# Query and key projections of two chunks by seven quarter products (Winograd's form of Strassen's scheme) in an attention kernel on one core

## The chip, the cores and the metric

The kernel runs on one core of one Trainium2 chip. The metric is the device time of one execution in microseconds; the median of the runs is given. A core has five engines with a queue each: TensorE (PE, matrix products; its weight loads are listed as PEld), VectorE (DVE), ScalarE (ACT), GpSimd (POOL) and SyncE (SP, which here only issues DMAs). An engine works through its queue in order and waits at an instruction whose semaphores aren't there yet. [...]

## The reference

The input is `x`, 4 batches of 1024 tokens with 512 features. It is normalised over its features and goes through an attention layer with 16 heads of 128 and through a product with rounding to FP8; both are added to `x`. Shortened:

```python
xn = layernorm(x)
q  = rope(rmsnorm(heads(xn @ Wq + bq), qn_w))
w  = softmax((xn @ Wcmp + bcmp) in groups of 4 tokens)
entries = weighted sums of xn over each group          # 256 per batch
ck = rope(rmsnorm(entries @ Wk + bk, kn_w));  cv = entries @ Wv + bv
sc = where(causal, q @ ck.T / sqrt(128), NEG)
ctx_sparse = softmax over the 8 largest of sc, times cv
lk = rope(rmsnorm(heads(xn @ Wlk + blk), kn_w));  lv = heads(xn @ Wlv + blv)
ctx_local = softmax(banded q @ [lk of the previous 128, lk of these 128].T) @ [lv, lv]
attn = ((ctx_sparse + ctx_local) / 2) @ Wo + bo
ffn  = (fp8(xn / 2) * 2) @ (fp8(input2 / 2) * 2)
out  = x + attn + ffn
```

All products but the FP8 one are fp32, and an fp32 product appears as two instructions with two weight loads.

## The kernel before, in words

The tokens are cut into NT = 32 chunks of 128 (eight per batch), the heads into NU = 8 pairs. A **unit** is one chunk with one pair of heads, so there are NN = 256 units, and unit `n` is chunk `n // 8`, pair `n % 8` (`place`). All weights stay in SBUF: `wqk_sb[u]` holds 256 query and 256 key columns of a pair, `wlv_sb[u]` the value columns, `wo_sb[u]` the rows of Wo.

The order of the instructions is written out by hand (`manual_schedule`): the main loop runs over `s`, and one turn of it does different stages of several units, so that each engine's queue has work of other units in front of what would have to wait:

- `queries(s+3)`: four products of 128x512 (K = 512 in four tiles; L606) give queries and keys in one PSUM bank, `qp`. Two banks alternate.
- `squares` and `spread`: ACT sums the squares of the four heads from `qp` (L321), POOL makes the reciprocal roots (L315, L316).
- `normalize(s+2)`: DVE multiplies `qp` by them and by the norm's weights into `th` (L634). `rotate` turns half of each head: one product on POOL (L337), one product, one subtraction and one addition on DVE (L339, L341, L342).
- `turn_keys(s+2)` and `fetch_keys(s+2)`: DVE transposes in 32x32 blocks (L687, L690), SP writes the result to DRAM in four DMAs (L695) and reads it back, turned, as `qT` and `lkT` (L705).
- `scores(s)`: q against the keys of the previous chunk, of this chunk and of the compressed entries (L754, L761, L764) into `sc`.
- `weigh(s)`: DVE masks and finds maxima (L786, L800), the eight largest (L807), the negated maximum of them (L809) and marks them (L812); ACT takes exponentials (L814, L822).
- `settle(s)`: DVE keeps the marked ones and sums (L830), bounds the sums from below (L839) and inverts them (L840); `divide(s)`: ACT multiplies (L847).
- `turn(s)`, `fetch(s)`: DVE transposes the probabilities (`probB`, L865), SP writes them to DRAM in one DMA (`pr`, L873) and reads them back in four (`probT`, L907).
- `values_of(s+1)` and `keep_values`: four products of 128x256 (L712), copied by ACT (`lv`, L724).
- `values(s-1)`: the probabilities against the values (L924); `keep_context(s-2)`: ACT copies them out (L939); `to_output(s-2)`: two products with `wo_sb` (L957) into a bank that sums a chunk's eight units; after the eighth DVE adds it to the chunk (L966) and SP stores it.

On PE a turn is: scores(s), queries(s+3), to_output(s-2), values_of(s+1), values(s-1). SP's queue holds in a turn: the write of `pr`, four writes of keys, four reads of `probT`, two reads of `qT` and `lkT`, and then what chunks need.

Work that belongs to a chunk is done in small steps within the turns: `chunk_prep` (layer norm, transposed tokens to DRAM, group weights and sums), `fetch_tokens` and `fetch_with_ones` (tokens back, turned; row 0 of the first K-tile is replaced by ones so that the bias comes with the product), `chunk_entries` (the compressed keys and values), `chunk_eight` with `quantize` (rounding on DVE and POOL, L287 to L298, and the FP8 product L588). The first eight units turn keys and probabilities on PE.

PSUM: two banks `qp`, two `sc`, two `pp` (values, FP8 product, entries), one `ctx`, one `out`.

Of the kernel before, what the change touches and what calls it, by code (L numbers as in the profile page):

```python
# [19 lines left out]
P = 128  # L20
# [18 lines left out]
def kernel(  # L39
# [34 lines left out]
    NN = NT * NU  # L74
    assert S // RATIO <= 2 * P and NU == 8 and HID == 512
# [10 lines left out]
    def scratch(name, shape=(P, 512), dtype=F32):  # L86
        return work.tile(list(shape), dtype, tag="scratch", name=name, bufs=2)

    def pp(name):
        return psum.tile([P, 512], F32, tag="pp", name=name, bufs=2)  # L90
# [5 lines left out]
    x_tiles, angles = {}, {}  # L96

    def load_x(t, purpose, extra=False):

        b, c = divmod(t, NCH)  # L100
        if extra:
            xt = scratch(f"x_{purpose}_{t}")
        else:
            xt = work.tile([P, HID], F32, tag="x", name=f"x_{purpose}_{t}")
        nc.sync.dma_start(xt, hidden[b, ts(c, P), :])
        x_tiles[purpose, t] = xt

    def load_angles(t):
        c = t % NCH
        cs = work.tile([P, ROPE], F32, tag="cs", name=f"cs_{t}")  # L110
        nc.sync.dma_start(cs, rope[ts(c, P), :])
        angles[t] = cs
# [10 lines left out]
    wqk_sb = [const.tile([P, KK, 512], F32, name=f"wqk_{u}") for u in range(NU)]  # L123
    wlv_sb = [const.tile([P, KK, 256], F32, name=f"wlv_{u}") for u in range(NU)]
    wo_sb = [const.tile([P, 2, HID], F32, name=f"wo_{u}") for u in range(NU)]

    def load_wqk(u, engine):
        for i, w in enumerate((Wq, Wlk)):
            engine.dma_start(
                wqk_sb[u][:, :, ts(i, 256)], w[:, ts(u, 256)].rearrange("(k p) n -> p k n", p=P)  # L130
            )
# [4 lines left out]
    def load_wo(u, engine):  # L136
        engine.dma_start(wo_sb[u], Wo[ts(u, 256), :].rearrange("(h p) n -> p h n", p=P))
# [13 lines left out]
    for k in range(KK):  # L151
        for i, w in enumerate((Wq, Wlk)):
            nc.sync.dma_start(wqk_sb[0][:, k, ts(i, 256)], w[ts(k, P), 0:256])
# [109 lines left out]
    def fold_first_row(u):  # L263
        w = wqk_sb[u]
        row = first_row.pop(u, None)
        if row is None:
# [3 lines left out]
                row, ident[:, 0:1].to_broadcast([P, P]), w[:, 0, :], start=True, stop=True  # L270
            )
        nc.vector.tensor_tensor(
            w, w, row.unsqueeze(1).to_broadcast([P, KK, 512]), ALU.subtract
        )
        for i, bias in enumerate((bq, blk)):
            nc.sync.dma_start(
                w[0:1, 0, ts(i, 256)], bias[ts(u, 256)].partition_broadcast(1)
            )

# [21 lines left out]
    w2_sb = const.tile([P, KK, HID], BF16, name="w2_sb")  # L301


    w2_raw = [wo_sb[NU // 2 + k][:, 0, :] for k in range(KK)]

    def round_w2():
        for k in range(KK):
            spare = wo_sb[NU // 2 + k][:, 1, :]
# [14 lines left out]
    def rotate(th, cs, nh, a, name, bb=None):  # L323
# [17 lines left out]
        nc.vector.tensor_tensor(x12[:, :, 0, :], a[:, :, 0, :], bb[:, :, 1, :], ALU.subtract)  # L341
        nc.vector.tensor_tensor(x12[:, :, 1, :], a[:, :, 1, :], bb[:, :, 0, :], ALU.add)  # L342


    GC = P // NE
    entries = {}
# [4 lines left out]
    def chunk_prep(t):  # L351
# [46 lines left out]
        log = work.tile([P, 1], F32, tag="log", name=f"log_{t}", bufs=1)  # L398
        row = work.tile([P, 2, BLK], F32, tag="row", name=f"row_{t}", bufs=1)
        red = work.tile([P, BLK // RATIO], F32, tag="red", name=f"red_{t}", bufs=1)  # L400
# [19 lines left out]
        if not t:  # L420
            add_tokens_here(row)
            return
# [21 lines left out]
        else:  # L444
            stores.append((pooled[g][i], few))
        yield "added"
# [31 lines left out]
    def turn_tokens_here(xt):  # L478
# [4 lines left out]
        xnT = work.tile([P, KK, P], F32, tag="xnT", name="xnT_0")  # L483
# [3 lines left out]
    def fetch_tokens(t):  # L487
        xnT = work.tile([P, KK, P], F32, tag="xnT", name=f"xnT_{t}")
# [5 lines left out]
        chunks[t] = xnT, xones[t % 2]  # L494


    xones = [const.tile([P, P], F32, name=f"xone_{i}") for i in range(2)]

    def fetch_with_ones(t):
        turned = tokens.pop(t).rearrange("i (b k) a j -> b i k (a j)", b=NB)  # L500
        for b in range(NB):
            lo = 0 if b else 1
            nc.sync.dma_start(
                xones[t % 2][b * BLK + lo : (b + 1) * BLK], turned[b, lo:, 0, :]
# [92 lines left out]
    def place(n):  # L597

        return divmod(n, NU)

    def queries(n):
        t, u = place(n)
        xnT, xone = chunks[t]
        qp = psum.tile([P, 512], F32, tag="qp", name=f"qp_{n}")
        for k in range(KK):
            nc.tensor.matmul(  # L606
                qp,
                xnT[:, k, :] if k or not t else xone,
                wqk_sb[u][:, k, :],
# [7 lines left out]
        ss = work.tile([P, 4], F32, tag="ss", name=f"ss_{n}")  # L617
        units[n] = {"qp": qp, "ss": ss}

    def squares(n, heads):  # L620
        w = units[n]
        for i in heads:
            square_sum(w["ss"][:, i : i + 1], w["qp"][:, ts(i, D)], f"{n}_{i}")
# [5 lines left out]
    def normalize(n):  # L629
        w = units[n]  # L630
        qp, r = w.pop("qp"), w["r"]
        th = work.tile([P, 4, D], F32, tag="th", name=f"th_{n}", bufs=1)
        for i in range(4):
            nc.vector.scalar_tensor_tensor(  # L634
                th[:, i, :],
                qp[:, ts(i, D)],
# [22 lines left out]
    def turn_keys_here(n):  # L659
# [4 lines left out]
        for i in range(4):  # L664
            nc.tensor.transpose(tq[:, ts(i, P)], th[:, i, :], ident)

# [7 lines left out]
    def key_tiles(n):  # L674
        w = units[n]
        qT = work.tile([P, NB, 2 * BLK], F32, tag="qT", name=f"qT_{n}", bufs=2)
        lkT = work.tile([P, NB, 2 * BLK], F32, tag="lkT", name=f"lkT_{n}", bufs=NU + 2)
# [3 lines left out]
    def turn_keys(n):  # L681
# [10 lines left out]
        )  # L692
        turned = dram.tile([NB, NB, BLK, 4 * BLK], F32, tag="qk", name=f"qk_{n}")
# [13 lines left out]
    def values_of(n):  # L707
        t, u = place(n)
        xnT = chunks[t][0]
        vp = pp(f"vp_{n}")  # L710
        for k in range(KK):
            nc.tensor.matmul(  # L712
                vp[:, 0:256],
# [7 lines left out]
    def keep_values(n):  # L721
        w = units[n]
        lv = work.tile([P, 2, D], F32, tag="lv", name=f"lv_{n}", bufs=NU + 2)
        nc.scalar.copy(lv.rearrange("p h d -> p (h d)"), w.pop("vp")[:, 0:256])  # L724
# [12 lines left out]
    def scores(n, h):  # L737
# [6 lines left out]
        if n == NN - 2:  # L744

            w.setdefault("sc", []).append(psum.tile([P, 512], F32, tag="qp", name=f"sc_{n}_{h}"))
# [6 lines left out]
        if c:  # L753
# [3 lines left out]
                units[n - NU]["lkT"][:, :, ds(h * BLK, BLK)],  # L757
# [6 lines left out]
        nc.tensor.matmul(sc[:, spa], q, ckT[:, 0:m], start=True, stop=True)  # L764
# [451 lines left out]
```

## Time and profile before

| | |
|---|---|
| median of 3 runs | 2642.6 us (2640.92 to 2643.14) |
| span of the profiled execution | 2641.7 us |
| PE busy | 2609.3 us, 11879 instructions |
| DVE busy | 2213.4 us, 8381 instructions |
| ACT busy | 1390.9 us, 5560 instructions |
| POOL busy | 786.2 us, 1128 instructions |
| DMA | 422.20 MB, 722252 packets |
| granted TensorE clock, mean | 0.999 |

The span reaches from the first to the last instruction of the profiled execution; the runs are timed without a profile. Busy times are the union of an engine's instructions; since products are pipelined and their ends are modelled, the distance from one start to the next says more about PE than the duration of one. A "releaser" is the instruction or DMA whose semaphore ended a wait. Some of the costliest groups (busy us, mean ns of one, idle time before them and what ended it):

```profile
L606 PE MATMUL qp<-wqk,xnT 128*128 128x512 f32 x1552 | 709.8, 593 | 3.0 <-DMA wqk<-in_L_attn_Wlk_dram 2.4
...
L847 ACT ACTIVATE prob<-prob,tot 128x256 f32<-128x256 f32 (+7 forms) x1024 | 382.0, 443 | 294.5 <-DVE tot L840 294.5
...
L957 PE MATMUL op<-wo,cT 128*128 128x512 f32 x1024 | 481.6, 593 | 4.2 <-ACT cT L939 4.2
L712 PE MATMUL vp<-wlv,xnT 128*128 128x256 f32 x2048 | 483.6, 379 | 0.0
...
L865 DVE STREAM_TRANSPOSE probB<-prob 128x512 f32<-128x512 f32 (+2 forms) x490 | 305.8, 629 | 11.5
...
L924 PE MATMUL cp<-probT,lv 128*128 128x128 f32 x1920 | 299.0, 276 | 6.4 <-DMA probT<-pr 4.9
```

### The profile page before, as it was taken

The page shows a single profiled execution, that of the slowest core. Times are in us where ns is not written, and L with a number is a line of the kernel's source. Part 1 is how long each engine was busy: PE and PEld are TensorE (multiplying, and loading weights), DVE is VectorE, ACT ScalarE, POOL GpSimd, SP SyncE. Part 2 cuts the span into 40 slices and gives each one's busy share as a digit, 9 for nine tenths or more (in the row PEclk, how much of TensorE's full clock was granted, in tenths as well). Part 3 has the DMA queues.
Part 4 walks back from the last instruction along what each step waited for, and adds up shares of the span by engine and source line. Part 5 has one row for each costly group of instructions (what it writes and reads, how often), then busy time and mean ns, then how long its engine had stood idle before and what let it go on. Part 6 is the DMA issues. An engine that isn't in the chain of part 4 may idle for free.

```text
span 2641.7 us, 46868 instructions
## 1 busy us (share of the span) xinstructions
PE 2609.3 (99%) x11879; PEld 1784.3 (68%) x11879; DVE 2213.4 (84%) x8381; ACT 1390.9 (53%) x5560; POOL 786.2 (30%) x1128
## 2 busy tenths in 40 slices
PE   8999999999999999999999999999999999999998
PEld 4666666776666666767766666667666666676776
DVE  6888888889888888888888888888888888877886
ACT  3545545555555555555555555555555555555555
POOL 3522323223332223232233322233323322322222
PEclk9999999999999999999999999999999999999999
DMA  8356556666655555666655555666665555566554
GB/s 255 110 156 162 151 145 175 171 176 158 164 143 154 162 155 156 169 173 170 166 157 144 158 149 158 177 164 164 171 176 147 150 148 153 147 168 171 159 152 110
DMA packets 722252, 422.20 MB, mean 160 GB/s; under 512 B 395823, under 2 KB 671552, under 8 KB 721984
## 3 DMA queue, kind: packets, MB, share of 16 engines
q1 hardware_dynamic: 721952, 419.20, 58.8%
q8 instruction: 97, 1.59, 0.3%
q14 instruction: 171, 1.40, 0.2%
q10 hardware_dynamic: 32, 0.02, 0.0%
HBM read 225.80 MB, written 193.20 MB: 159 GB/s over the span
## 4 chain that ended last, share of the span: by engine, by line
PE 84%; DVE 7%; ACT 3%; DMA 3%; SPq 2%; issue 1%; POOL 0%; ACTq 0%; DVEq 0%
PE qp L606 28%; PE op L957 14%; PE vp L712 14%; PE cp L924 13%; PE sc L764 5%; PE sc L761 4%; PE sc L754 4%; ACT prob L847 1%; ACT prob L814 1%; PE fp L588 1%; DVE sc L786 1%; DVE probB L865 1%; PE ep L536 1%; SPq L695 1%; DVE taken L812 1%
## 5 line engine op out<-in xcount | busy, mean ns | idle before, releaser
L606 PE MATMUL qp<-wqk,xnT 128*128 128x512 f32 x1552 | 709.8, 593 | 3.0 <-DMA wqk<-in_L_attn_Wlk_dram 2.4
L814 ACT ACTIVATE prob<-sc,neg 128x256 f32<-128x256 f32 (+1 forms) x512 | 235.9, 461 | 773.3 <-DVE taken L812 744.0
L606 PEld LDWEIGHTS qp<-wqk,xnT 128*128 128x128 f32 x1552 | 295.0, 190 | 372.5 <-issue 368.8
L847 ACT ACTIVATE prob<-prob,tot 128x256 f32<-128x256 f32 (+7 forms) x1024 | 382.0, 443 | 294.5 <-DVE tot L840 294.5
L712 PEld LDWEIGHTS vp<-wlv,xnT 128*128 128x128 f32 x2048 | 389.0, 190 | 161.3 <-issue 116.2
L957 PE MATMUL op<-wo,cT 128*128 128x512 f32 x1024 | 481.6, 593 | 4.2 <-ACT cT L939 4.2
L712 PE MATMUL vp<-wlv,xnT 128*128 128x256 f32 x2048 | 483.6, 379 | 0.0
L337 POOL TENSOR_TENSOR rb<-th,cs 128x256 f32<-128x256 f32 x256 | 203.8, 796 | 740.0 <-DVE th L634 733.2
L786 DVE CUSTOM_DVE_ANT_0 sc<-sc,mask_b 128x256 f32<-128x256 f32 (+1 forms) x512 | 211.6, 414 | 172.7 <-PE sc L764 162.7
L957 PEld LDWEIGHTS op<-wo,cT 128*128 128x128 f32 x1024 | 193.6, 190 | 229.8 <-issue 186.8
L865 DVE STREAM_TRANSPOSE probB<-prob 128x512 f32<-128x512 f32 (+2 forms) x490 | 305.8, 629 | 11.5
L315 POOL TENSOR_SCALAR r<-ss 128x4 f32<-128x4 f32 x256 | 61.9, 242 | 843.3 <-ACT junk L321 840.6
L924 PE MATMUL cp<-probT,lv 128*128 128x128 f32 x1920 | 299.0, 276 | 6.4 <-DMA probT<-pr 4.9
L321 ACT ACTIVATE junk<-qp 128x128 bf16<-128x128 f32 x1024 | 278.6, 272 | 28.9 <-PE qp L614 4.5
L924 PEld LDWEIGHTS cp<-probT,lv 128*128 128x128 f32 x1920 | 272.8, 191 | 25.4 <-issue 9.3
L634 DVE SCALAR_TENSOR_TENSOR th<-qp,r,norm_w 128x128 f32<-128x128 f32 x1024 | 286.1, 342 | 0.7 <-POOL r L316 0.4
L316 POOL TENSOR_TENSOR r<-r,nhalf 128x4 f32<-128x4 f32 x256 | 265.6, 1037 | 21.4
L830 DVE SCALAR_TENSOR_TENSOR prob<-taken,prob 128x128 f32<-128x128 bf16 (+7 forms) x512 | 186.4, 365 | 98.1 <-ACT prob L822 96.6
L606 PE MATMUL qp<-wqk,xone 128*128 128x512 f32 x496 | 258.3, 602 | 0.9 <-DMA xone<-xb_dram 0.7
L924 PE MATMUL cp<-probT,cv 128*128 128x128 f32 x1536 | 255.1, 275 | 0.0
L764 PE MATMUL sc<-ckT,qT 128*128 128x96 f32 (+7 forms) x1024 | 226.4, 303 | 0.0
L924 PEld LDWEIGHTS cp<-probT,cv 128*128 128x128 f32 x1536 | 212.7, 192 | 0.0
(141 smaller groups left out, 3674.9 us busy)
## 6 DMA issues: line engine op xcount, KB each, us to landing
pr<-probB SPq DMA_DIRECT2D x125, 512.0 KB
probT<-pr SPq DMA_DIRECT2D x500, 128.0 KB
qk<-thb SPq DMA_DIRECT2D x992, 64.0 KB
pr<-probB SPq DMA_DIRECT2D x96, 384.0 KB
probT<-pr SPq DMA_DIRECT2D x384, 96.0 KB
qT<-qk SPq DMA_DIRECT2D x248, 128.0 KB
lkT<-qk SPq DMA_DIRECT2D x248, 128.0 KB
x_norm<-_attn_hidden_states_dram SPq DMA_DIRECT2D x32, 256.0 KB
```

Of the source, the lines that this page charges most:

```text
L316: nc.gpsimd.tensor_tensor(r, r, nhalf[: ss.shape[0], 0:n], ALU.pow)
L321: nc.scalar.activation(junk[: src.shape[0]], src, AF.Square, accum_out=acc)
L606: nc.tensor.matmul(qp, xnT[:, k, :] if k or not t else xone, wqk_sb[u][:, k, :], start=(k == 0), stop=(t > 0 and k == KK - 1),)
L634: nc.vector.scalar_tensor_tensor(th[:, i, :], qp[:, ts(i, D)], r[:, i : i + 1], norm_w[:, i // 2, :], ALU.mult, ALU.mult,)
L712: nc.tensor.matmul(vp[:, 0:256], xnT[:, k, :], wlv_sb[u][:, k, :], start=(k == 0), stop=(k == KK - 1),)
L764: nc.tensor.matmul(sc[:, spa], q, ckT[:, 0:m], start=True, stop=True)
L786: nc.vector.tensor_tensor_reduce(sc[h][:, loc], sc[h][:, loc], mask_b[:, loc], -1.0, TAKEN, ALU.add, ALU.min, neg[h][0],)
L814: nc.scalar.activation(probs[h][:, loc], sc[h][:, loc], AF.Exp, bias=neg[h][0], scale=-1.0, accum_out=tot[:, h, 0:1],)
L847: nc.scalar.mul(probs[h][:, cols], probs[h][:, cols], tot[:, h, part : part + 1])
L865: nc.vector.transpose(pb[:, :, ds(h * g, g), :], prob[:, parts[0] * P : (parts[-1] + 1) * P].rearrange("p (g b i) -> p b g i", b=NB, i=BLK),)
L924: nc.tensor.matmul(blocks(cp[:, h, :]), v, probT[:, :, h * len(parts) + i - parts[0], :], start=(i == parts[0]), stop=(i == parts[-1]),)
L957: nc.tensor.matmul(op, cT[:, h, :], wo_sb[u][:, h, :], start=(u == 0 and h == 0), stop=(u == NU - 1 and h == 1),)
```

## The change

From chunk 4 on (unit FIRST = 32) chunks are taken in pairs: units alternate between the two chunks of a pair, with the same pair of heads, so that unit `2q` and `2q+1` use the same weights. Their queries and keys are a product of two chunks by 512 features with 512 features by (256 query + 256 key columns). Each side is cut in 2 x 2 quarters, A by chunk and half of K, B by half of K and queries or keys, and the four quarters of the result come from seven products of quarters instead of eight. A product of quarters (`product`) is two K-tiles of 128x256.

- **Combined weights**: four differences of weight quarters for each pair of heads are made once, by POOL, in units 9 to 24 (`combine_weights`), and stored in DRAM. For each pair of units they are loaded again, four DMAs of 256 KB (`load_combined`), into the places in SBUF of a quarter of the weights that is no longer used.
- **Sums of tokens**: four sums per pair of chunks on POOL (`sum_tokens`).
- **Products**: p1, p6, p5 and p3 go into one PSUM region, one after the other, each adding to what stands there; between them ACT copies the state out into `th` (`keep1`, `keep6`, `keep5`, `keep3`). p2 goes to another bank, p7 and p4 to a third, where p4 is added to p7. DVE adds p2, p7 and p7 + p4 to parts of `th` (`sum2`, `sum7`, `sum4`). Even turns hold p1, p2, p6, p7, odd ones p5, p3, p4. Squares and normalisation read `th` (SBUF) from then on, not PSUM.
- **Room**: the `wo` rows are loaded for each unit, later for each pair of units (512 KB), into two buffers; `lkT`, `lv`, `th` and the token tiles come from hand-managed pools; the value products and the context share one bank; FP8 products and entries share the bank of p2. `to_output` moves ahead of `settle` in program order, on PE between p2 or p5 and the next product.
- **Vector work**: the two additions of the rotation go from DVE to POOL; the negated maxima of both heads are made by one instruction instead of two; the lower bound of the sums (L839) is left out but for the first chunk of a batch.
- Steps of chunk preparation, entries, FP8 products and loads of tokens get new turns. In `values` the rows of entries that don't exist yet are left out.

The diff, cut to its core:

```diff
+    combined = [
+        dram.tile([4, P, 512], F32, tag=f"combined_{u}", name=f"combined_{u}", bufs=1)
+        for u in range(NU)
+    ]
+    def combine_weights():
+        one, two = (v.rearrange("p h d -> p (h d)") for v in th_tiles[2:])
+        for u in range(NU):
+            (b11, b12), (b21, b22) = (
+                [flat(wqk_sb[u][:, j, i]) for i in range(2)] for j in range(2)
+            )
+            for i, (to, a, b) in enumerate(
+                ((one, b12, b11), (two, b22, one), (one, b21, two), (two, b22, b12))
+            ):
+                nc.gpsimd.tensor_tensor(to, a, b, ALU.subtract)
+                stores.append((combined[u][(0, 1, 3, 2)[i]], to))
+                yield
+    def load_combined(q, which):
+        for i in which:
+            at = ring[(4 * (q - FIRST // 2) + (2, 0, 1, 3)[i]) % len(ring)]
+            nc.sync.dma_start(at, combined[q % NU][i])
+            loaded[q, i] = at.rearrange("p (k n) -> p k n", k=2)
+    def sum_tokens(p):
+        (a11, a12), (a21, a22) = ((b[:, 0:3:2, :], b[:, 3:5, :]) for b in (x_bufs(2 * p), x_bufs(2 * p + 1)))
+        s1, s2, s3, s4 = token_sums
+        op = nc.gpsimd.tensor_tensor
+        op(s1, a21, a22, ALU.add)
+        op(s2, s1, a11, ALU.subtract)
+        op(s3, a11, a21, ALU.subtract)
+        op(s4, a12, s2, ALU.subtract)
...
-        nc.vector.tensor_tensor(x12[:, :, 0, :], a[:, :, 0, :], bb[:, :, 1, :], ALU.subtract)
-        nc.vector.tensor_tensor(x12[:, :, 1, :], a[:, :, 1, :], bb[:, :, 0, :], ALU.add)
+        adder = nc.gpsimd if nh > 1 else nc.vector
+        adder.tensor_tensor(x12[:, :, 0, :], a[:, :, 0, :], bb[:, :, 1, :], ALU.subtract)
+        adder.tensor_tensor(x12[:, :, 1, :], a[:, :, 1, :], bb[:, :, 0, :], ALU.add)
...
+    regions = [v[:, 0:256] for v in (qk_banks[0], pp_bank, qk_banks[1])]
+    def product(i, a, b, first=True):
+        for k in range(2):
+            nc.tensor.matmul(regions[i], a[k], b[:, k, :],
+                start=first and k == 0, stop=k == 1, skip_group_check=not first)
+    def p1(q):
+        p, u = divmod(q, NU)
+        xa, one = chunks[2 * p]
+        product(0, (one, xa[:, 1, :]), wqk_sb[u][:, 0, 0])
+    def keep1(q):
+        take_th(2 * q)
+        nc.scalar.copy(half(2 * q, 0), regions[0])
+    def p2(q):
+        product(1, both(chunks[2 * p][0][:, 2:4, :]), wqk_sb[u][:, 1, 0])
+    def p6(q):
+        product(0, both(token_sums[1]), loaded.pop((q, 1)), False)
+    def p7(q):
+        product(2, both(token_sums[2]), loaded.pop((q, 2)))
+    def p5(q):
+        product(0, both(token_sums[0]), loaded.pop((q, 0)), False)
+    def p3(q):
+        product(0, both(token_sums[3]), wqk_sb[u][:, 1, 1], False)
+    def p4(q):
+        product(2, both(chunks[2 * p + 1][0][:, 2:4, :]), loaded.pop((q, 3)), False)
+    def add_to(n, i, what):
+        nc.vector.tensor_tensor(half(n, i), half(n, i), what, ALU.add)
...
         for_unit(s, (scores, 0), (scores, 1))
         for_unit(s - 2, (keep_context,))
+        if odd:
+            for_pair(q, (p5,), (keep5,))
+        elif s != FIRST - 4:
+            for_pair(q, (p1,), (keep1,), (p2,))
         for_unit(s, (weigh,))
-        for_unit(s + 3, (queries,))
+        if s + 3 < FIRST:
+            for_unit(s + 3, (queries,))
+        if even:
+            for_pair(q + 1, (load_combined, (1, 2)))
+        else:
+            for_pair(q + 1, (load_combined, (0, 3)))
+        for_pair(*((q, (sum7,)) if odd else (q - 1, (sum4,))))
         for_unit(s + 2, (normalize,))
+        for_unit(s - 2, (to_output,))
+        if even:
+            for_pair(q, (p6,), (keep6,))
         for_unit(s, (settle,))
         for_unit(s, (divide,))
         for_unit(s + 2, (go_on_rotating,), (end_rotation,))
+        if even:
+            for_pair(q, (sum2,))
+        for_unit(s + 1, (values_of,))
+        if odd:
+            for_pair(q, (p3,), (keep3,))
         if by_dma(s):
             turn(s)
         for_unit(s + 3, (squares, (0, 1, 2, 3)), (spread,))
-        for_unit(s - 2, (to_output,))
-        for_unit(s + 1, (values_of,))
         for_unit(s - 1, (values,))
+        for_pair(q, (p4 if odd else p7,))
```

## Prediction

> **What bounds the kernel now.** I read the engine table first, then the chain of waits in a stretch of ordinary units, then PE's weight loads, the waits, and the DVE and SP timelines of the same stretch.
>
> ```profile
> span 2641.7 us, 46868 instructions
> ...
> PE 2609.3 (99%) x11879; PEld 1784.3 (68%) x11879; DVE 2213.4 (84%) x8381; ACT 1390.9 (53%) x5560; POOL 786.2 (30%) x1128
> ...
> q1 hardware_dynamic: 721952, 419.20, 58.8%
> ```
>
> PE is never without work, but DVE at 84% is close behind it, and the DMA engines are 59% taken. The chain of waits shows what a unit is made of (start, us, what):
>
> ```profile
> 1514.56 3.46 PE qp L606 x8
> 1518.02 1.72 PE op L957 x4
> 1519.74 1.73 PE vp L712 x8
> 1521.46 1.34 PE cp L924 x12
> 1522.80 0.24 PE sc L754 x2
> ...
> 1524.19 3.46 PE qp L606 x8
> ```
>
> One unit after the other is on the chain with PE alone: 3.46 + 1.72 + 1.73 + 1.34 and 1.38 for scores are 9.63 us, and every eighth unit has 0.86 for the FP8 product (L588). An fp32 product is two instructions, so the x8 are four products. A 512-wide instruction takes 3.46/8 = 0.43 us, a 256-wide one 1.73/8 = 0.216: half, so narrow products cost nothing extra here, although each has its own weight load:
>
> ```profile
> 1519.58 1.49 PEld L712 LDWEIGHTS vp<-wlv,xnT 128*128 128x128 f32 x7 [0.24 <-issue]
> ```
>
> Seven loads in 1.49 us keep pace with seven products of 0.216. Time that PE is spared is therefore time of the kernel, until another wait is as late. The waits (us in total, times, longest) of PE and of SP's queue, and SP's timeline, tell how near that one is:
>
> ```profile
> PE cp L924 <- DMA probT<-pr: 4.9, 9, 0.9
> ```
>
> ```profile
> SPq L873 <- DVE probB L865: 754.5, 219, 7.1
> ```
>
> ```profile
> 1511.25 0.54 SPq L873 DMA_DIRECT2D pr<-probB  x1
> 1511.90 1.86 SPq L695 DMA_DIRECT2D qk<-thb  x4
> 1513.89 1.81 SPq L907 DMA_DIRECT2D probT<-pr  x4
> ```
>
> From the scores' end (1514.4 in this period) DVE and ACT need some 7 us to the transposed probabilities (L865); then SP writes them to DRAM, writes four parts of the keys, and reads them back in four parts; PE takes them up in the next unit (L924). PE waits for that only 4.9 us in all. But the margin is small: I took, for the 245 units that go through DRAM, the last landing of the fetch (the last update of its semaphore before the semaphore is issued again) and the start of the unit's first context product. From unit 32 on the margin is 1.74 us in the mean, 0.86 its standard deviation, and 0.1 to 0.5 in the worst.
>
> **The change part by part.** *Products.* For 112 pairs of units (32 to 255) 2 x 8 instructions of 0.43 go (6.92 us) and 7 products x 2 K-tiles x 2 = 28 of 0.216 come (6.05). That is 0.87 us a pair, 97 us in all. Upper side of the new cost: should every product expose one weight load (0.19, mean of L712's), 7 x 0.19 x 112 = 149 us would eat it all; lower side: nothing. I take nothing: at L712 to L924 the row goes from one tile to another, past a DMA wait, in the usual step (1.73 for eight, and the next start is at 1521.46).
>
> *The bank that is copied out between.* ACT makes four copies of 128x256 a pair; the row of lv (L724) is 366 ns, so 0.73 us a unit, and ACT goes from 5.4 us a unit (1390.9/256) to 6.2 of about 9.2. PE waits if a copy is late. After the first product come p2 and the output product (0.87 + 1.72), after the third the unit's values (1.73), after the second the rest of the unit; ACT's queue holds only the two context copies (0.64) ahead of the first and third copies, and the second stands behind the exponentials, some 4.1 us after the scores, when its product is done (4.3). Hidden, with 1 to 5 us of cover. If that cover goes, the delay is on PE in full; bound: one 0.37 copy at each of four places, 4 x 0.37 x 112 = 166 us; I take 0.
>
> *DVE.* Three sums of 128x256 from PSUM come per pair (L547, 397 ns): 0.60 us a unit. Out go L341 and L342 (0.292 + 0.284, now on POOL), one of two L809 (0.153), and L839 in seven of eight units (0.362 in the mean). DVE falls by about 0.45 us a unit. The first sum of a unit stands between the top-8 and the normalisation, where DVE afterwards waits for ACT's exponentials anyway (L830 <- ACT L822, 96.6 us in 248 waits, 0.39 each); so on the way to L865 only L809 and L839 count, both as a gain.
>
> ```profile
> 1498.88 1.13 DVE L839 TENSOR_SCALAR tot<-tot 128x4 f32<-128x4 f32 x1
> ...
> 1508.70 0.17 DVE L839 TENSOR_SCALAR tot<-tot 128x4 f32<-128x4 f32 x1
> ```
>
> In 52 of 256 units L839 takes about 1.1 us instead of 0.17, each time beside a POOL operation (L294 or L298 at most) of the FP8 rounding. [...]
>
> *POOL.* Two additions of 128x128 per unit aren't in the trace; L337's rows bound one from 0.325 (128x64) to 0.796 (128x256); by their slope I take 0.48, 0.96 for both. They must end before the keys' transposes (L687), and in front of these DVE has L865, 1.15 to 1.5 us: hidden, and if not, the key writes that stand ahead of the fetch on SP come late by the rest, up to 0.4. Once in 16 units four sums of the tokens (0.80 each, 3.2 us) follow the reciprocal roots; the next POOL work of the path comes some 4 us later. Combining the weights is 32 POOL operations of 128x512 (L583, 1.27 us) in units 9 to 24, two a unit on an engine 30% busy: hidden, bounded by 41 us.
>
> *DMA and SP.* Each pair loads 4 x 256 KB of combined weights and 512 KB of Wo: 176 MB, with the first units about 197 MB on top of 419. At 58.8% for 419 MB that makes 28 points more, near 87%. SP issues 2.5 more of some 13 a unit, at 0.47 us (1.86 for four): 1.2 us a unit. SP waited 3.4 us on average (754.5/219) before the write of the probabilities; the loads are issued in that gap, and in the shorter unit about 1.8 us of it are left. Where a chunk's own loads (up to 8 issues) fall into the same gap, the write is late.
>
> *What comes closer.* The path from the scores to the fetch lasts as long as before, but PE arrives sooner: between scores and context stood 3.46 + 1.72 + 1.73; now it is three products (2.6) and 3.45 in even units, two (1.73) and 3.45 in odd ones, 1.30 less on average; and the unit before is 0.43 shorter. 1.73 us of a mean margin of 1.74 are gone. I went through the 221 margins in order, took off 1.73, gave back 0.15 and each unit's own L839, and let a unit that waited give its wait to the next (its scores come later by as much, and its successor's fetch does not). Added waits: 24 us with no other delay, 36 with 0.25 us more delay in every unit from SP and DMA, 50 with 0.5, 86 with 1.0, 131 with 1.5. I take 0.25, for a fifth of the units at about 1 us.
>
> Sum: 2641.7 - 97 + 36 = 2581, plus 5 for the shared bank of FP8 products and second product, and the burst on POOL (32 chunks x some 0.15): 2586. The profiled span lies 0.9 under the runs' median, so 2586 stands for the runs too. Own range 2565 to 2620 (waits of 15 to 75).
>
> **The rivals.** *All of it is kept*: the relief of DVE brings the probabilities out half a microsecond sooner, beyond L809 and L839. For: DVE is the most loaded engine after PE. Against: L865 waits for ACT's division, not for DVE alone (ACT L847 <- DVE L840, 294.5 us). Waits 10, time about 2550. Chance 0.13.
>
> *The trip through DRAM takes over* (the other side): SP and the DMA queue make the write of the probabilities late in most units. For: 87% DMA share, and the combined weights stand ahead of the write on the one SP queue. Against: the gap of 3.4 us. It decides once the delay is above 1.1 us in every unit, where the waits are 94; at 1.5 the time is 2642 - 97 + 131 = 2676. Chance 0.24.
>
> *The products gain nothing*, because weight loads show through at half of the seven: 97 - 75 is 22, less 24 of waits, 2644. Chance 0.06.
>
> **How the numbers follow.** Forecast 0.57, the rivals 0.13, 0.24 and 0.06. A change under 0.2% (5 us) can't be told from none here. Faster: 0.57 + 0.13 and nothing of the others, 0.70; same 0.06; slower 0.24. The range goes from 2548 (all kept, no wait) to 2650, which leaves out most of the third case, about 0.16, and a little below.
>
> **What would show it.** Right: p1 to p7 in steps of 0.216 us; a wait of PE's context product for probT of tens of us, the largest PE wait; DVE busy time down by some 100 us; SP's wait for probB down by half or more. Wrong: PE waiting for ACT's copies (bank not free), a product step above 0.25, or the wait for probT above 95 us.

## The result and the profile after

The changed kernel takes 2908.07 us in the median (four runs, 2892.23 to 2917.45), the kernel before 2642.87 in the same session: the ratio is 1.1001 (95% interval 1.0964 to 1.1038; later intervals stand in brackets), 265 us slower. The forecast was 2586, its range 2548 to 2650: wrong in sign, and outside the range. The profiled span is 2912.7, so the views below stand for the runs.

The page of the changed kernel: span, busy time of the engines, the DMA queue (packets, MB, share of 16 engines), and the chain of waits by engine and by line:

```profile
span 2912.7 us, 50814 instructions
...
PE 2718.6 (93%) x13170; PEld 2132.2 (73%) x13205; DVE 2160.6 (74%) x7725; ACT 1567.3 (54%) x6000; POOL 1076.2 (37%) x1714
...
q1 hardware_dynamic: 825168, 615.91, 74.0%
...
PE 51%; DMA 20%; DVE 13%; ACT 6%; SPq 6%; issue 3%; POOL 0%; ACTq 0%; DVEq 0%; POOLq 0%
PE vc L1139 13%; PE qk L744 12%; DMA pr<-probB 12%; DMA probT<-pr 7%; PE out L1170 7%; PE vc L922 6%; SPq L1122 4%; PE sc L974 3%; PE sc L971 3%; ACT prob L1055 3%; PE sc L964 3%; DVE sc L995 2%; PE pp L744 2%; DVE prob L1037 2%; DVE taken L1019 1%
```

The same line of the kernel before:

```profile
PE 84%; DVE 7%; ACT 3%; DMA 3%; SPq 2%; issue 1%; POOL 0%; ACTq 0%; DVEq 0%
```

PE had 84% of the chain before; now it has 51%, and a fifth of the span is waiting for DMA, 19 points of it for the two legs of the probabilities' trip through DRAM. The waits of PE and of SP's queue (us, times, longest):

```profile
PE vc L1139 <- DMA probT<-pr: 152.9, 98, 5.3
...
PEld vc L1139 <- DMA probT<-pr: 47.7, 29, 4.3
```

```profile
SPq L1122 <- DMA pr<-probB: 255.3, 189, 4.1
SPq L1081 <- DVE probB L1073: 208.6, 83, 7.6
SPq L1081 <- DVE thb L896: 186.8, 72, 5.6
```

The context product (L1139; L924 before) waited 4.9 us in all, and now 152.9, with 47.7 more at its weight load. SP idles less ahead of the write of the probabilities (754.5 us before, 395.4 in the two rows of L1081 now) and more behind it, until the write has landed (255.3 us; before, at L907, as follows).

```profile
SPq L907 <- DMA pr<-probB: 24.2, 37, 1.4
```

The chain of waits of one unit that PE waited for (start, us, what):

```profile
1513.03 4.97 DMA pr<-probB
1518.07 0.30 SPq L1122
1518.41 0.44 SPq L1122
1518.89 0.44 SPq L1122
1519.37 2.09 DMA probT<-pr
1521.60 1.70 PE vc L1139 x8
1523.30 1.06 PE qk L744 x4
```

The write needs 4.97 us; PE takes the data up 0.14 us after the last fetch is there. SP's timeline of the same stretch shows what stands ahead of that write and runs beside it:

```profile
1510.84 0.62 SPq L169 DMA_DIRECT2D wo<-in_L_attn_Wo_dram  x1
1511.50 0.95 SPq L352 DMA_DIRECT2D wqk<-combined  x2
1512.56 0.38 SPq L1180 DMA_DIRECT2D out_dram<-x  x1
1513.03 0.38 SPq L1081 DMA_DIRECT2D pr<-probB  x1
```

A megabyte of loads was issued in the 2.2 us before it, and the DMA engines are 0.95 busy while it is under way. Over units 32 to 255 (221 of them, from the trace's issue and landing times) the trip's pieces are, in us in the mean:

| | before | after |
|---|---|---|
| end of the scores to transposed probabilities | 8.25 | 8.03 |
| then to the issue of the write | 0.11 | 0.56 |
| issue of the write to its landing | 2.75 | 3.93 |
| then to the issue of the fetch | 0.20 | 0.08 |
| issue of the fetch to its landing | 4.30 | 4.24 |
| units whose product starts under 0.3 us after the landing | 10 | 105 |

While the write is under way, the DMA engines are busy for 0.66 of the time before and 0.85 after (packet times of the traces, the same units).

To see where PE's time went I took the distance from each PE instruction's start to the next, less what its columns need at the full clock, and sorted the rest by cause (from 30 us on to 25 us before the end):

| us | before | after | difference |
|---|---|---|---|
| at the full clock, no waits | 2523.3 | 2418.2 | -105.1 |
| waits | 23.8 | 203.4 | +179.6 |
| extra while the granted clock is halved | 3.1 | 98.7 | +95.6 |
| extra where the number of active rows changes | 0 | 94.7 | +94.7 |
| other | 35.7 | 41.7 | +6.0 |

The products do save what was forecast (some 8 of the 105 are product records missing from the trace). Waits, the halved clock and the changing rows cost 370. The last two of these had no term in the forecast. The granted clock is the share of its full speed that TensorE is given. The stretch with the clock halved, in windows (window, length, busy us and instructions of PE, PEld, DVE, ACT, POOL, granted clock, DMA share, GB/s):

```profile
176.00:179.60 3.60, 1.99 (x12) 1.62 (x12) 0.77 (x2) 0.03 (x1) 0.42 (x2) 1.00 0.92 271
179.60:183.00 3.40, 3.40 (x15) 3.06 (x15) 0.36 (x2) 0.90 (x3) 3.23 (x4) 0.50 0.87 204
183.00:187.00 4.00, 4.00 (x10) 1.71 (x9) 3.44 (x21) 1.43 (x6) 0.87 (x2) 1.00 0.88 209
```

and PE's timeline of the same place (start, us, instructions, the wait ahead of them in brackets):

```profile
168.03 0.40 PE L971 MATMUL sc<-lkT,qT 128*128 128x128 f32 x2
168.27 0.35 PE L974 MATMUL sc<-ckT,qT 128*128 128x64 f32 x2
...
177.62 0.71 PE L1139 MATMUL vc<-probT,lv 128*128 128x128 f32 x4 [2.07 <-DMA probT<-pr]
...
180.37 0.63 PE L971 MATMUL sc<-lkT,qT 128*128 128x128 f32 x2
180.79 0.53 PE L974 MATMUL sc<-ckT,qT 128*128 128x64 f32 x2
```

A wait of 2.07 us is followed by 3.4 us at a clock of 0.50, in which the product of L971 (two instructions) takes 0.42 us to the next start, and 0.24 a turn earlier. All scores of this turn take 2.61 us, a turn earlier 1.46: the 2 us of waiting cost over 1 us more behind them.

### The profile page after: what moved, and what is told of

It is laid out like the page before. It is cut to its first block, busy times and chain, and to the rows that moved or that the text cites. A ratio compares the mean times of both kernels' runs of the same rounds, so it can differ in the third digit from the quotient of the medians.

```text
span 2912.7 us, 50814 instructions
## 1 busy us (share of the span) xinstructions
PE 2718.6 (93%) x13170; PEld 2132.2 (73%) x13205; DVE 2160.6 (74%) x7725; ACT 1567.3 (54%) x6000; POOL 1076.2 (37%) x1714
## 4 chain that ended last, share of the span: by engine, by line
PE 51%; DMA 20%; DVE 13%; ACT 6%; SPq 6%; issue 3%; POOL 0%; ACTq 0%; DVEq 0%; POOLq 0%
PE vc L1139 13%; PE qk L744 12%; DMA pr<-probB 12%; DMA probT<-pr 7%; PE out L1170 7%; PE vc L922 6%; SPq L1122 4%; PE sc L974 3%; PE sc L971 3%; ACT prob L1055 3%; PE sc L964 3%; DVE sc L995 2%; PE pp L744 2%; DVE prob L1037 2%; DVE taken L1019 1%
## 5 line engine op out<-in xcount | busy, mean ns | idle before, releaser
L429 POOL TENSOR_TENSOR rb<-th,cs 128x256 f32<-128x256 f32 x256 | 194.1, 758 | 955.0 <-DVE th L842 954.9
L1170 PE MATMUL out<-wo,cT 128*128 128x512 f32 x1024 | 486.2, 597 | 12.4 <-DMA wo<-in_L_attn_Wo_dram 7.8
L922 PE MATMUL vc<-wlv,tokens 128*128 128x256 f32 x2048 | 487.5, 381 | 4.3 <-ACT lv L934 4.3
L1139 PE MATMUL vc<-probT,lv 128*128 128x128 f32 x1920 | 335.8, 297 | 155.7 <-DMA probT<-pr 152.9
L922 PEld LDWEIGHTS vc<-wlv,tokens 128*128 128x128 f32 x2048 | 391.7, 191 | 120.8 <-issue 69.6
L744 PE MATMUL qk<-wqk,wqk 128*128 128x256 f32 x1736 | 457.8, 387 | 0.0
L1021 ACT ACTIVATE prob<-sc,neg 128x256 f32<-128x256 f32 (+1 forms) x510 | 234.9, 461 | 399.2 <-DVE taken L1019 395.4
L1139 PEld LDWEIGHTS vc<-probT,lv 128*128 128x128 f32 x1920 | 277.0, 199 | 224.8 <-issue 151.1
L744 PEld LDWEIGHTS qk<-wqk,wqk 128*128 128x128 f32 x1736 | 319.0, 192 | 90.1 <-issue 48.5
L1139 PE MATMUL vc<-probT,cv 128*128 128x128 f32 (+3 forms) x1536 | 309.6, 304 | 0.0
L413 ACT ACTIVATE junk<-th 128x128 bf16<-128x128 f32 x896 | 275.1, 307 | 21.2
L744 PE MATMUL qk<-wqk,tokens 128*128 128x256 f32 x896 | 263.0, 420 | 0.2 <-DVE th L842 0.2
L1139 PEld LDWEIGHTS vc<-probT,cv 128*128 128x128 f32 (+3 forms) x1536 | 234.7, 200 | 32.7 <-issue 4.0
L842 DVE SCALAR_TENSOR_TENSOR th<-th,r,norm_w 128x128 f32<-128x128 f32 x896 | 255.8, 348 | 0.0
L1037 DVE SCALAR_TENSOR_TENSOR prob<-taken,prob 128x96 f32<-128x96 bf16 (+7 forms) x512 | 233.3, 464 | 19.1 <-ACT prob L1029 10.8
L974 PE MATMUL sc<-ckT,qT 128*128 128x160 f32 (+5 forms) x1020 | 231.2, 309 | 0.0
```

Source lines behind the costliest of these rows:

```text
L413: nc.scalar.activation(junk[: src.shape[0]], src, AF.Square, accum_out=acc)
L744: nc.tensor.matmul(regions[i], a[k], b[:, k, :], start=first and k == 0, stop=k == 1, skip_group_check=not first,)
L842: nc.vector.scalar_tensor_tensor(th[:, i, :], src[i], r[:, i : i + 1], norm_w[:, i // 2, :], ALU.mult, ALU.mult,)
L922: nc.tensor.matmul(vp, xnT[:, k, :], wlv_sb[u][:, k, :], start=(k == 0), stop=(k == KK - 1),)
L1037: nc.vector.scalar_tensor_tensor(probs[h][:, spa], taken[:, h, 0:m], TAKEN_FROM, probs[h][:, spa], ALU.is_ge, ALU.mult, accum_out=tot[:, h ...
L1139: nc.tensor.matmul(blocks(cp[:, h, :]), v[0:rows], probT[0:rows, :, h * len(parts) + i - parts[0], :], start=(i == parts[0]), stop=(i == p ...
```

## The experiments

Two suspects at first: the loads, and the partial rows of the context products, which the forecast had passed over. Each was taken out of the changed kernel, and each put into the old one alone. All times are medians beside the kernel before in the same session (2642.2 to 2642.9).

**All 128 rows.** In `e1_rows` the context products take all rows, and small memsets on POOL keep the probabilities of absent entries at zero:

```diff
...
+        elif n >= FIRST and n % 2 == 0:
+            for prob in probs:
+                nc.gpsimd.memset(prob[:, 2 * P + m : 2 * P + m + NE], 0.0)
...
-                    v, rows = cv[i - 2], min(P, m - P * (i - 2))
+                    v, rows = cv[i - 2], P
```

> The changed kernel with all 128 rows in every context product again (the rows of entries that don't exist yet are multiplied by probabilities set to zero on POOL, two small memsets in every second unit). Theory R (a product of fewer rows costs PE about 0.1 us at each change of the row count, 95 us in the trace of the changed kernel: 82 from 380 us on and 13 before): those steps go back to 0.112 us, the time falls by 40 to 95 us, to 2815 to 2870; part of it comes back as waits, since PE reaches the probabilities sooner. Theory D alone (only the late write of the probabilities sets the time): the 95 us turn into waits, 2890 or more.

2893.27 us, ratio 1.094 [1.0913, 1.0967]: 15 us less than the changed kernel, which is within the 25 us that its runs differ by. The rows' extra falls from 94.7 us to 0.2, but the waits rise from 203 to 288: a PE that is faster only arrives earlier at data that isn't there.

**No loads.** `e2_noloads` makes the loads of combined weights only for the first places and of Wo only up to unit 35, so that later units compute with wrong weights; only its time counts:

```diff
-        engine.dma_start(w, Wo[ts(u, 256), :].rearrange("(h p) n -> p h n", p=P))
+        if n < FIRST + 4:
+            engine.dma_start(w, Wo[ts(u, 256), :].rearrange("(h p) n -> p h n", p=P))
...
-            nc.sync.dma_start(at, combined[q % NU][i])
+            if 4 * (q - FIRST // 2) + (2, 0, 1, 3)[i] < len(ring):
+                nc.sync.dma_start(at, combined[q % NU][i])
```

> The changed kernel with the loads of combined weights only for the first six places and of Wo only up to unit 35; later pairs compute with what is there, so the output is not the reference's. Theory D (the loads stand ahead of the write of the probabilities in the DMA queue): the write lands after 2.75 us again instead of 3.93, PE idles for less than 60 us after unit 32 instead of 172, and the granted clock comes back to 0.99, since the halved stretches follow the waits; time 2660 to 2740. If the loads are not the cause: 2860 or more and the clock still 0.97.

2725.42 us, 1.0317 [1.03, 1.0334]. The loads are the larger part: 183 us go with them, and the write lands after 2.79 us again.

**The rows alone, on the kernel before.** `e3_before_rows`:

```diff
-                    v = cv[i - 2]
+                    v, rows = cv[i - 2], min(P, m - P * (i - 2))
...
-                    v,
-                    probT[:, :, h * len(parts) + i - parts[0], :],
+                    v[0:rows],
+                    probT[0:rows, :, h * len(parts) + i - parts[0], :],
```

> The old kernel with one edit of the change, the context products with only the rows of entries that exist. Theory R: 192 of 256 units have four changes of the row count, 0.1 us each, 77 to 95 us: 2720 to 2740. If fewer rows are free, as the prediction had it: 2643.

2732.08 us, 1.0338 [1.0322, 1.0353]: leaving out rows of zeros costs 90 us where PE is the bound. The context products of one unit in PE's timeline, before and then in this kernel:

```profile
157.82 0.61 PE L924 MATMUL cp<-probT,lv 128*128 128x128 f32 x4
158.27 0.39 PE L924 MATMUL cp<-probT,cv 128*128 128x128 f32 x2
158.49 0.61 PE L924 MATMUL cp<-probT,lv 128*128 128x128 f32 x4
...
159.16 0.40 PE L754 MATMUL sc<-lkT,qT 128*128 128x128 f32 x2
```

```profile
158.55 0.61 PE L924 MATMUL cp<-probT,lv 128*128 128x128 f32 x4
159.09 0.48 PE L924 MATMUL cp<-probT,cv 64*128 64x128 f32 x2
159.50 0.71 PE L924 MATMUL cp<-probT,lv 128*128 128x128 f32 x4
...
160.56 0.50 PE L754 MATMUL sc<-lkT,qT 128*128 128x128 f32 x2
```

From the first start to the scores 1.34 us before, 2.01 now; a product of 64 rows takes 0.41 us instead of 0.22, and the pair of products next to it loses 0.1 to 0.2. The scores' first step grows by 0.1. That is 0.77 us a unit; the 128 units whose last part has 32 or 64 rows make 98, near the 90. A product of 96 rows steps as one of 128 does (0.11 us an instruction), so it is 128 units and not the 192 that were expected.

**The loads alone, on the kernel before.** `e4_before_loads` issues as many bytes as the change does from unit 32 on, at like places of the turn, writing Wo's rows over themselves:

```diff
+        if s >= 28:
+            for h in range(2):
+                v = (u + 4) % NU
+                nc.sync.dma_start(wo_sb[v][:, h, :], Wo[ds(v * 256 + h * P, P), :])
...
+        if s >= 32 and s % 2:
+            load_wo((u + 3) % NU, nc.sync)
```

> The old kernel with DMA loads of the same sizes and at the same places as in the change (two of 256 KB a unit after the queries, 512 KB at the end of every second unit), which load Wo's rows again over themselves. Theory D: the write of the probabilities lands later by about 1.2 us in the mean; the margin of 1.74 takes most of it, waits of 15 to 45 us and with the clock 2660 to 2720. If the traffic is harmless: at most 2650.

2844.49 us, 1.0758 [1.073, 1.0786]: 202 us, over twice what I had expected. Its DMA queue and the waits of PE and SP:

```profile
q1 hardware_dynamic: 816672, 594.87, 73.1%
```

```profile
PE cp L924 <- DMA probT<-pr: 132.0, 76, 4.4
```

```profile
SPq L907 <- DMA pr<-probB: 241.8, 176, 4.1
```

The old kernel shows the picture of the changed one with nothing of the products in it: the write is issued 0.81 us after the transposes and lands 4.22 us later, PE waits 174 us in all (24 before), and the halved clock costs 53 (3 before). No wait of PE for the added loads themselves is listed.

**Half of that traffic.** `e11_before_half` loads one 256 KB part for each unit and one for every second:

```diff
-            for h in range(2):
-                v = (u + 4) % NU
-                nc.sync.dma_start(wo_sb[v][:, h, :], Wo[ds(v * 256 + h * P, P), :])
+            v = (u + 4) % NU
+            nc.sync.dma_start(wo_sb[v][:, s % 2, :], Wo[ds(v * 256 + s % 2 * P, P), :])
...
```

> The old kernel with half the traffic of e4: one load of 256 KB a unit and 256 KB at the end of every second unit. If the loads cost once the margin of the probabilities is used up: less than half of e4's 202 us, 2660 to 2710. If they cost in proportion to their bytes: about 2743.

2673.11 us, 1.0103 [1.0086, 1.0121], at 507.04 MB and 68.7%; the write lands in 3.19 us. The first 88 MB cost 31 us, the second 88 MB 171: the price is not in proportion to the bytes.

**Neither rows nor loads.** `e5_rows_noloads` is both of the first two edits at once.

> The changed kernel with full rows and with the loads left out from unit 36 on (output not the reference's, as in e2). What is left is the seven products themselves and the first 32 units. If the loads and the rows are the whole loss: the steps of changed rows (90 us in e2) go; PE comes 0.4 us a unit sooner to the probabilities, so about half comes back as waits and clock: 2640 to 2690, idle PE after unit 32 80 to 120 us. If something else in the change costs (copies between the products, POOL), the waits would be behind qk or out, not behind probT.

2671.55 us, 1.0106 [1.0089, 1.0123]. Against `e1_rows` the loads cost 222 us, and against `e2_noloads` the rows cost 54. But without rows and loads the products still show no gain: PE's own work is 98 us less than before, its waits are 109 more, and the halved clock costs 12. The trip through DRAM is still PE's largest wait, but no longer nearly all of it; the output product (L1175) now waits for ACT's copy of the context (4.2 us before):

```profile
PE vc L1144 <- DMA probT<-pr: 56.5, 68, 2.9
...
PE out L1175 <- ACT cT L1160: 18.9, 21, 4.6
```

**More margin.** If the trip is the bound, then work moved from behind the wait to ahead of it must pay. `e6_rows_last` is `e1_rows` with the turn's last products (p7, p4) ahead of the context products:

```diff
+        for_pair(q, (p4 if odd else p7,))
         for_unit(s - 1, (values,))
-        for_pair(q, (p4 if odd else p7,))
```

> The changed kernel with full rows (e1) and the last product of the turn (p4 or p7) put before the context products instead of behind them. Theory D: PE asks for the probabilities 0.86 us later, so e1's waits (242 us) fall by 80 to 130 us and the halved clock with them: 2750 to 2820. If the waits are bound by throughput of the DMA queue and not by the margin: 2870 or more.

2863.93 us, 1.0832 [1.0792, 1.0872]: 29 us better than `e1_rows`, less than expected, since the write lands no sooner than there (4.33 us, 4.18 in `e1_rows`). The same move without the loads, `e9_noloads_last`:

> e5 (full rows, no loads from unit 36 on; output not the reference's) with the last product of the turn put before the context products, 0.86 us more margin. If the seven products save PE's time as reckoned and only the trip of the probabilities takes it back: waits after unit 32 fall from 86 to 20 to 40 us, 2605 to 2630, that is 155 or so per 16 units at full width and 143 to 146 at the narrow end. If the products themselves are slower in the stream: 2660 or more.

2642.89 us, 0.9997 [0.9988, 1.0006]: again 29 us, and short of the 2605 to 2630 that were expected.

**Is it the order on SP's queue or the engines' time?** `e7_act_queue` is `e6_rows_last` with the loads issued by ACT at the end of the turn; `e8_after_fetch` issues them on SP right behind the fetch of the probabilities, ahead of that of queries and keys. The core of the first edit (the calls also move to the end of the turn, and Wo's loads with them):

```diff
-            nc.sync.dma_start(at, combined[q % NU][i])
+            nc.scalar.dma_start(at, combined[q % NU][i])
...
```

> e6 with the loads of combined weights and (from unit 34 on) of Wo issued from ACT at the end of a turn, so that they are in another queue than the write of the probabilities. If the order in one queue makes the write late: issue delay back to 0.1 and landing to about 3 us, waits under 80 us, 2640 to 2720. If the 16 engines' time itself is short (75% taken): landing stays near 4, no gain over e6.

> e6 with all these loads on SP right behind the fetch of the probabilities and ahead of the fetch of the keys. Order theory: the write lands after about 3 us, waits under 100 us, 2660 to 2740; the keys arrive 1.3 to 2 us later, their margin of 2.8 us (median in the changed kernel) pays for it. If the keys become late instead: waits of the scores for qT or lkT of 50 us or more.

2916.08 us, 1.1036 [1.1007, 1.1065], and 2906.15 us, 1.0992 [1.0967, 1.1018]. With the loads on ACT's queue the write lands in 3.13 us, but the fetch takes 5.87 instead of 4.23; the DMA engines are 0.88 busy during the fetch, 0.68 in `e6_rows_last`, and during the write 0.78 instead of 0.88. Behind the fetch, the wait moves to the scores, which need the queries:

```profile
PE sc L964 <- DMA qT<-qk: 147.5, 82, 4.3
PE vc L1142 <- DMA probT<-pr: 36.2, 36, 2.9
```

In these three places, from two queues, the same bytes came with a delay of something that PE needs: the write (4.33 us in `e6_rows_last`), the fetch (5.87 us) or the queries (147.5 us of waits). `e7_act_queue` changes the queue and the place in the turn together, so the queue's own part isn't shown.

**The first 32 units.** Up to the scores of unit 32 `e9_noloads_last` takes 36 us more than the kernel before (379.5 against 343.3 from the first scores), though its products there are the old ones. `e10_first_units` is `e9_noloads_last` with one thing more left out: it loads Wo only for units 0 and 1 and makes and stores the combined weights of two of the eight pairs:

```diff
-        if n < FIRST + 4:
+        if n < 2:
...
-        for u in range(NU):
+        for u in range(2):
```

> e9 with the first 32 units freed of what the change adds to them: Wo loaded only for units 0 and 1, weights combined and stored for two of eight pairs of heads (output not the reference's). If the 38 us that the first 32 units lose (381 against 343 us between the first and the 32nd scores) come from these loads, stores and POOL operations: 25 to 40 us less than e9. If they come from the new order of instructions and chunk work: no difference to e9.

2607.25 us, 0.9859 [0.9844, 0.9874]: 36 us less than `e9_noloads_last`; up to the scores of unit 32 it is some 40 us less. This is the only kernel with the products that beats the old one, and it leaves out what its expectation says; of the 97 us it keeps 35. PE's waits are still 49.5 us above those of the kernel before, and the halved clock costs 9 more. By now the trip through DRAM is not the largest wait:

```profile
PE out L1175 <- ACT cT L1160: 19.4, 20, 3.8
...
PE vc L1144 <- DMA probT<-pr: 17.4, 20, 2.6
```

**The vector edits alone.** `e12_before_vector` is the kernel before with the rotation's additions on POOL, one negation for two, and L839 for the first chunk of a batch alone:

```diff
+        adder = nc.gpsimd if nh > 1 else nc.vector
+        adder.tensor_tensor(x12[:, :, 0, :], a[:, :, 0, :], bb[:, :, 1, :], ALU.subtract)
...
-        nc.vector.tensor_scalar(tot, tot, 1e-9, None, ALU.max)
+        if not c:
+            nc.vector.tensor_scalar(tot, tot, 1e-9, None, ALU.max)
```

> The old kernel with the vector edits of the change alone: rotation's two additions on POOL, one negation for both heads, no lower bound of the sums but in a batch's first chunk. PE bounds the old kernel, so the time stays: 2635 to 2645; DVE's busy time falls by 200 to 260 us, and the probabilities are turned 0.2 to 0.4 us earlier. If the two additions on POOL hold the keys up: 2650 or more.

2640.45 us, 0.999 [0.9981, 0.9999]. The engines' line of its page:

```profile
PE 2608.3 (99%) x11879; PEld 1786.1 (68%) x11879; DVE 2002.5 (76%) x7389; ACT 1403.0 (53%) x5560; POOL 1003.2 (38%) x1640
```

DVE is spared 211 us, the probabilities come 0.54 us sooner, the margin grows from 1.74 to 2.14 us; and since PE is the bound, the time hardly changes. It is the fastest of the kernels that compute the whole reference, by 2 us, which its interval hardly sets apart from none.

## Why the prediction was wrong, and where it was right

**The step that failed** is the delay from SP and DMA, "I take 0.25, for a fifth of the units at about 1 us". It measured 0.45 us more before the issue and 1.18 more until the landing, 1.63 together. The fetch gave back 0.18 (0.12 and 0.06). The prediction's table had also given back 0.15 and each unit's own L839 (0.33 in the mean over these units), 0.48 in all, for vector work that falls away; of that the trace shows 0.22. In the table's own terms the delay is therefore 1.63 - 0.18 + 0.26 = 1.71 us, where 0.25 was taken. The prediction had the cause on paper: 87% DMA share (it came to 74.0%, in a longer span), and a rival in which "the trip through DRAM takes over" with 0.24. Against it stood "the gap of 3.4 us" in SP's queue. That gap answers when a write can be issued, not when it lands; the write's landing, 2.75 us in the trace, was treated as a constant while 197 MB were added beside it.

**The table itself held for the wait that it was made for.** Redone from the 221 margins, it gives some 150 us at a delay of 1.71; PE's wait of the context product for probT is 152.9 us, 148 more than before. In `e5_rows_noloads`, where the trip is 0.12 us shorter than before and so 0.36 longer than the table took it, the table gives some 43; the wait is 56.5, 36.2 of it from 380 us on. The rest of the 86 us that PE waits there from 380 us on (4 before) stands mostly at places that had no term, or too small a one: the output product for ACT's copy of the context (13.6), the FP8 product for DVE's sum from the bank that it shares with p2 (10.5).

**The clock wasn't in the sum.** The mean granted clock was 0.999 in a kernel whose PE waited 24 us in all, and the prediction priced no change of it. With 203 us of waits it is 0.966, at a cost of 96 us; in `e5_rows_noloads`, with 133, 0.994.

**The partial rows weren't in the sum.** The edit was described, but no row of the profile was looked up for it. Alone it costs 90 us (`e3_before_rows`), without the loads 54, and within the changed kernel at most about 15 (`e1_rows`), where the waits grow by 85 us when the rows' 95 go. The savings can't be added up one by one for the same reason.

**The first units.** The combining on POOL was put as "hidden, bounded by 41 us", and the stores and the loads of Wo in these units had no term. Together they cost 36 us. Which share of it is the combining on POOL, and which the loads of Wo, the one run doesn't tell.

**What held.** The products step by 0.216 us as taken, 97 us less PE work (`e1_rows` has 97.3). No wait of PE for ACT's copies of the shared bank is listed. An addition on POOL takes 0.457 us (0.48 taken). Of the marks for "right", the product step and the context product's wait for probT as PE's largest came true, though at 153 us and not tens; SP's wait ahead of the write fell from 754.5 to 395.4 us in the two rows of L1081, not quite by half. The mark for "wrong", that wait of PE above 95 us, came true as well. DVE's busy time fell by 53 us, not 100: the vector edits give 211 (`e12_before_vector`; the prediction's 1.05 us a unit would make 268), so the new sums and what else DVE does take back 158, where three sums a pair had been put at 0.60 x 224 = 134. The rival in which weight loads show through is refuted by the steps.

**DVE beside POOL.** At the normalisation (L842) of the changed kernel 3 of 1024 instructions took over 0.5 us (1.00 in the mean, the median 0.35), each beside a POOL operation. Of the 32 executions of L839 that stay (L1047), 23 take 0.57 us beside the rotation's product on POOL, and of the 256 merged negations (L1017) 22, each beside a POOL operation, take 0.83 us in the mean instead of 0.17. One of them in DVE's timeline, and POOL's beside it (start, us, what):

```profile
150.07 0.96 DVE L1017 TENSOR_SCALAR neg_spa<-top 128x2 f32<-128x2 f32 x1
```

```profile
149.74 1.26 POOL L336 TENSOR_TENSOR th<-wqk,th 128x512 f32<-128x512 f32 x1
```

The negation ends with the POOL subtraction (151.03 and 151.00 us). At the negation this is small: 22 x 0.66 = 15 us of DVE time. But L839, the one place that the prediction names, wasn't the only one, in the kernel before either. The instruction that keeps the marked probabilities (L830; L1037 now) is longer beside POOL too, and its row grew (busy us, mean ns of one):

```profile
L830 DVE SCALAR_TENSOR_TENSOR prob<-taken,prob 128x128 f32<-128x128 bf16 (+7 forms) x512 | 186.4, 365 | 98.1 <-ACT prob L822 96.6
```

```profile
L1037 DVE SCALAR_TENSOR_TENSOR prob<-taken,prob 128x96 f32<-128x96 bf16 (+7 forms) x512 | 233.3, 464 | 19.1 <-ACT prob L1029 10.8
```

At 128 columns it takes 0.50 us in the mean when a POOL TENSOR_TENSOR overlaps it, which is then nearly always the rotation's product (L429), and 0.28 when none does; in the kernel before, where that product (L337) overlaps it about as often, it took 0.31 at 128 columns, but at 32 columns 0.60 when a POOL TENSOR_TENSOR was running as it started, and 0.21 when none was. The mean grew by 0.1 us, with two such instructions a unit: 0.2 us a unit more on the way from the scores to the probabilities, about the size of the 0.26 by which the vector work's gain fell short; in `e12_before_vector` the instruction takes 358 ns and the gain is 0.54. No run tried whether the one makes up the other.

## What to carry to other kernels

Before trading products for loads, list the small dependent transfers whose landing PE waits for, and price their landing time under the new DMA share (here 2.75 us at 58.8% and 3.93 at 74.0%), not only their place in the issuing queue. When PE has no slack to give, its savings pay only as far as the margin of the next chain reaches; here 97 us of fewer products met a margin of 1.74 us a unit, and PE's earlier arrival alone was reckoned at 1.73 of it. And a shape that looks like less work (fewer rows, 90 us more in `e3_before_rows`) needs its own row in a profile before it is taken as free.

## What the runs showed of the hardware

**Rows.** An fp32 product is two instructions (L971 and L974 above: x2 for one product). With 32 or 64 active rows among products of 128, one such instruction steps to the next start in 0.21 us (median) instead of 0.11 (`e3_before_rows`), with 96 rows in 0.11; its duration is 321 ns against 275, with 96 rows 274. The products next to the narrow ones step later by some 0.1 us.

**The clock.** In the changed kernel, of 40 PE waits of 2 us or more 33 had a halved stretch begin during the wait or within 3.5 us of its end (10 and 23), of 55 shorter ones (0.5 to 2 us) 5. A stretch lasts 3.41 us or multiples of it, 196 us in all after the first 30 us.

**DMA.** With 88 MB more (58.8% to 68.7% mean share) the kernel before lost 31 us, with 176 MB (73.1%) 202. At 73 to 74% the write of 384 or 512 KB landed 1.2 to 1.5 us later than the 2.75 us of the kernel before. With the loads issued from ACT at the end of the turn SP's fetch took 5.87 us (`e7_act_queue`), and 4.23 with them on SP's queue (`e6_rows_last`).

Not tried: a kernel that loads combined weights once for two pairs of chunks, which would have about half of the added traffic.
